# Folding key totals to 16 rows by a third accumulating transfer, stacking them half as wide, and giving the first value projection another bank

## The chip, the cores and the metric

The kernel runs on one core of one Trainium2 chip. The metric is the device time of one launch in microseconds (us), lower is better. Matmuls run on TensorE (PE in the profile), elementwise work on VectorE (DVE), exponentials and copies on ScalarE (ACT), masks on GpSimd (POOL), which also issues the accumulating transfers; SyncE (SP) issues the other transfers. Each engine works through a queue of its own in order, and the engines wait for each other through semaphores.

## The reference

`x` has the shape (32, 256, 32, 32) in float32. It is normalised per group, projected to queries, keys and values with 8 heads of 32 channels, and each of the 1024 positions attends to the positions strictly before it. The result is added to `x`.

```python
xf = _gn(x).reshape(B, C, S)                        # B=32, C=256, S=1024, 32 groups of 8 channels
q = einsum('oc,bcs->bos', q_w, xf) + q_b[None, :, None]
kv = einsum('oc,bcs->bos', kv_w, xf) + kv_b[None, :, None]
k, v = kv[:, :256], kv[:, 256:]                     # then split into 8 heads of 32
mask = tril(ones((S, S)), -1)
scores = einsum('bhqd,bhkd->bhqk', q, k) / sqrt(32)
attn = softmax(where(mask == 0, -10000.0, scores))
attn = where(mask == 0, 0.0, attn)
out = einsum('bhqk,bhkd->bhqd', attn, v)            # back to (B, 256, 32, 32)
return x + out
```

## The kernel before, in words

The kernel works through 32 batch elements, called batches here. A batch is ten *visits*: two groups of four heads, five visits for each group. A visit (`scores`) computes transposed score products for four heads into three PSUM tiles, two long ones `sT` and one short one `tri`, and ACT writes their exponentials to SBUF as `e` (two instructions on L443) and `eh` (L446). POOL then zeroes the forbidden parts (`mask`, L388). One visit later PE multiplies the exponentials by the values (`values`, tile `acc`, L472), and DVE adds the exponential tiles of several visits together (`add_keys`, L490), always into the `e` tile of the group's first or second visit. So each batch leaves four tiles of key totals, numbers n = 0 to 3: two groups by two halves of 512 queries. Each has 128 rows of partial totals and 4 x 512 columns (heads by queries).

The softmax denominator is the sum over those 128 rows. The kernel gets it like this:

- `fold(b, n, rows)` (L505): POOL issues an accumulating transfer that adds rows `rows` to `2 * rows` of the total onto rows 0 to `rows`. The first fold leaves 64 rows, the second leaves 32. A fold waits until the one before it on the same tile has landed.
- `stack(b, n)` (L511): SP copies the 32 remaining rows to partitions 32n to 32n + 31 of one tile `folded`.
- `sum_folded(b, heads)` (L518, L519): per head, DVE transposes the 128 x 512 slice in 32 x 32 blocks into `turned` and sums runs of 32 into `rows`. Four heads make four transposes and four sums a batch.
- `invert` (L547 to L559) takes reciprocals and writes them to DRAM, `spread_inverses` (L573) reads them back to the tile `rb`, spread over the partitions, and `finish` (L598 to L607) scales, adds bias and residual, and stores.

The `e` tiles of the first two visits of each group, where the totals stand, are taken from a ring of four buffers (tag `e0`). The buffer of a total is therefore written again by ACT exactly ten visits later, at the same visit of the next batch, and ACT must wait there until every fold and every stack of the old total has landed. The total n = 3 stands in the `e` tile of visit 6 of its batch, so ACT needs it back at visit 16, which is visit 6 of the next batch.

The order is written by hand. For each visit number i the main loop emits `scores(i)`, the first part of `values` of visit i - 1, the list `at[i]`, the second part of `values`, `add_keys`, and the list `after[i]`. Tables give the visits, counted from the batch's first: `SUMS` for the first fold of each n (the second fold comes one visit later), `STACK` for the stack, `PROJECT` and `PREPARE` for the next batch's projections and normalisation, `LOAD` for the input of the batch after that. A visit's tables can thus reach beyond 10, into the next batch.

Three pieces of machinery matter below. First, `with_scores(ahead)` makes SP wait for the semaphore `bank_free[0]`, which PE raises early in the score products of this visit, or of a visit ahead: the four input transfers `x` of visit 5 (L113) are tied in pairs, the first pair to visit 5's scores and the second to visit 6's. Second, POOL waits for the semaphore `begun` before the first fold of n = 1, and ACT raises it between its `e` and `eh` exponentials of visit 7. Third, ten-odd instructions of the next batch's normalisation share POOL's queue with folds and masks: the gather `eight` (L212), `rstd` (L250) and `shift` (L254); ACT's `xn` (L269) waits for `shift`.

A projection takes a PSUM bank either through `room`, half of an `sT` tile, or through `lone`, the bank of `acc`.

Of the kernel before, what the change touches and what calls it, by code (L numbers as in the profile page):

```python
# [17 lines left out]
P = 128  # L18
HD = 32
CPG = 8  # L20
HALF = 512
# [5 lines left out]
HALFBANK = HALF // 2  # L27
SHORT = 3 * P
ROW = 64
KEYS = 64  # L30


@with_exitstack
def tile_norm_attention_residual(
# [19 lines left out]
    nc = tc.nc  # L54
    B, C, H, W = x.shape
    S = H * W
    NG = C // P
    NB = S // P
    NH = S // HALF
# [22 lines left out]
        out=avg, in_=avg, pattern=[[-CPG, P // CPG], [0, CPG]],  # L82
# [3 lines left out]
        out=avg, in_=avg, pattern=[[CPG, P // CPG], [0, CPG]],  # L86
# [17 lines left out]
    def unshifted():  # L104
        live = {}
        bank_free = [tc.alloc_semaphore(f"bank_free_{k}") for k in range(2)]
        begun = tc.alloc_semaphore("begun")
        xpool = tc.alloc_tile_pool(name="xpool", bufs=4)
# [193 lines left out]
        def projections(b):  # L302

            def qk(n, g, hf, *bank):
                return lambda: project_qk(b, g, n, hf, *bank)

            def v(n, *bank):
                return lambda: project_v(b, n, *bank)

            early = [lone] if b == 0 else []  # L310
            return [
                qk(0, 0, 0, *early), qk(1, 0, 0), qk(0, 0, 1, *early), v(0), qk(1, 0, 1), qk(0, 1, 0, lone),
                qk(1, 1, 0), v(1), v(2), v(3), qk(0, 1, 1), qk(1, 1, 1, lone),
            ]

# [183 lines left out]
        def fold(b, n, rows):  # L499
            total = live["sum", b, *divmod(n, NH)]  # L500
            if (n, rows) == (1, HD):
                nc.gpsimd.drain()
            if (n, rows) == (1, 2 * HD):
                nc.gpsimd.wait_ge(begun, b + 1)
            nc.gpsimd.dma_start(out=total[:rows], in_=total[rows : 2 * rows], accum_op=ALU.add)  # L505

        def stack(b, n):
            if n == 0:
                live["folded", b] = work.tile([P, 4, HALF], F32, tag="folded", bufs=1, name=f"folded_{b}")
            total = live.pop(("sum", b, *divmod(n, NH)))  # L510
            nc.sync.dma_start(out=live["folded", b][n * HD : (n + 1) * HD], in_=total[:HD])  # L511

        def sum_folded(b, heads):
            if heads.start == 0:
                live["rows", b] = small.tile([P, ROW], F32, tag="rows", name=f"rows_{b}")
            for j in heads:
                turned = small.tile([P, HALF], F32, tag="turned", bufs=1, name=f"turned_{b}_{j}")
                nc.vector.transpose(turned, live["folded", b][:, j, :])  # L518
                nc.vector.tensor_reduce(  # L519
                    live["rows", b][:, j * HALF // HD : (j + 1) * HALF // HD],  # L520
                    turned.rearrange("p (k r) -> p k r", r=HD), AX.X, ALU.add,
                )

        def sum_keys(pd, e, of, start=True, stop=True):
            for j in range(4):
# [52 lines left out]
        def invert_here(b, n, within=slice(0, HALF)):  # L578


            if ("rb", b) not in live:
                live["rb", b] = work.tile([P, 4, HALF], F32, tag="folded", bufs=1, name="rb_last")
# [68 lines left out]
        N = NG * len(VISITS)  # L651
# [48 lines left out]
        at, after = {}, {}  # L700

        def when(i, f, where=at):
            where.setdefault(i, []).append(f)
# [16 lines left out]
        PROJECT = (-5, -4, -2, -3, 0, 1, 1, -1, 2, 4, 3, 6)  # L720
        PREPARE = (-12, -11, -10, -10, -9, -8, -7, -6, -4, -4, -3)
        SUMS = (4, 6, 8, 11)
        STACK = (6, 9, 11, 14)
        LOAD = 5
        SPREAD = (1, 1, 3, 4)
        FINISH = (N + 11, N + 11, N + 12, N + 13)
# [3 lines left out]
        with tc.manual_schedule(engines={ENG.PE, ENG.Activation, ENG.DVE, ENG.Pool, ENG.SP}):  # L730
# [11 lines left out]
                norm_channels(0, g)  # L742
            norm_mean(0)
            keep_busy(6, HD)
            odd = work.tile([P, 4, HALF], F32, tag="folded", bufs=1, name="less_mean")[:, 0, :]
# [32 lines left out]
            for b in range(B):  # L778
                first, last = b * N, b == B - 1
# [13 lines left out]
                if not last:  # L793
                    for n in every:
                        v = first + SUMS[n]
                        when(v, lambda b=b, n=n: fold(b, n, 2 * HD), at if n == 0 else after)
                        when(v + 1, lambda b=b, n=n: fold(b, n, HD), after)
                        when(first + STACK[n], lambda b=b, n=n: stack(b, n), at if n else after)
                    late = b == B - 2
                    v = first + N + (4 if late else 5)  # L800
                    when(v, lambda b=b: sum_folded(b, every[:2]), after)
                    when(v + 1, lambda b=b: sum_folded(b, every[2:]), after)
                    when(v + 2, lambda b=b: invert(b))
# [212 lines left out]
```

## Time and profile before

| what | value |
|---|---|
| median of 3 runs | 1808.08 us (1803.84 to 1809.35) |
| profiled execution, its own time | 1806.47 us |
| its span | 1803.3 us |
| granted TensorE clock | 0.999 |
| busy share PE / DVE / ACT / POOL | 99% / 93% / 82% / 46% |
| accumulating transfers from POOL | 124 of 512 KB and 124 of 256 KB |
| stack transfers from SP | 124 of 256 KB |

The profile is of one execution. A row of the timeline gives the start and the duration in us, the engine, the line, the operation, `out<-in` with buffer numbers left out, and in brackets how long the engine stood idle before it and which instruction ended that; SPq is SP's queue of transfers, whose duration is that of the issue. A row of the groups has the number of instructions, the busy time in us, and the mean of one in ns.

### The profile page before, as it was taken

The page shows a single profiled execution, that of the slowest core. Times are in us where ns is not written, and L with a number is a line of the kernel's source. Part 1 is how long each engine was busy: PE and PEld are TensorE (multiplying, and loading weights), DVE is VectorE, ACT ScalarE, POOL GpSimd, SP SyncE. Part 2 cuts the span into 40 slices and gives each one's busy share as a digit, 9 for nine tenths or more (in the row PEclk, how much of TensorE's full clock was granted, in tenths as well). Part 3 has the DMA queues.
Part 4 walks back from the last instruction along what each step waited for, and adds up shares of the span by engine and source line. Part 5 has one row for each costly group of instructions (what it writes and reads, how often), then busy time and mean ns, then how long its engine had stood idle before and what let it go on. Part 6 is the DMA issues. An engine that isn't in the chain of part 4 may idle for free.

```text
span 1803.3 us, 82014 instructions
## 1 busy us (share of the span) xinstructions
PE 1782.8 (99%) x37208; PEld 983.7 (55%) x37208; DVE 1682.6 (93%) x1852; ACT 1469.8 (82%) x1736; POOL 833.2 (46%) x935
## 2 busy tenths in 40 slices
PE   8999999999999999999999999999999999999998
PEld 5555555555555555555555555555555555555554
DVE  3789999999999999999999999999999999999996
ACT  5888888888888888888888888888888888888884
POOL 2445644444444444544544444545444444445541
PEclk9999999999999999999999999999999999999999
DMA  2566776666766767767667666676676676666662
GB/s 69 105 118 129 150 134 137 137 138 136 149 127 138 144 134 148 129 134 143 131 145 146 129 137 142 137 148 128 136 147 131 145 143 131 138 140 136 131 120 86
DMA packets 92771, 240.23 MB, mean 133 GB/s; under 512 B 26272, under 2 KB 27792, under 8 KB 76544
## 3 DMA queue, kind: packets, MB, share of 16 engines
q0 software_dynamic: 17360, 100.58, 39.0%
q1 hardware_dynamic: 74912, 134.28, 26.3%
q8 instruction: 292, 4.78, 1.1%
q14 instruction: 63, 0.52, 0.1%
q10 hardware_dynamic: 144, 0.07, 0.0%
HBM read 69.90 MB, written 34.95 MB: 58 GB/s over the span
## 4 chain that ended last, share of the span: by engine, by line
PE 57%; DVE 32%; issue 5%; DMA 3%; ACT 2%; DVEq 0%; SPq 0%; POOL 0%; ACTq 0%
DVE e L490 20%; PE acc L472 17%; PE pp L180 14%; PE tri L381 10%; PE sT L381 8%; PE ppv L180 7%; DVE turned L518 3%; DVE rows L519 3%; DVE rb L601 2%; DMA rb<-inverses 2%; DVE num L598 2%; ACT eh L446 2%; DVE st L196 1%; PE pd L526 1%; DVE mv L219 1%
## 5 line engine op out<-in xcount | busy, mean ns | idle before, releaser
L443 ACT ACTIVATE e<-sT 128x1024 f32<-128x1024 f32 x640 | 620.8, 1022 | 209.1 <-PE sT L381 204.3
L381 PE MATMUL tri<-q,k 32*64 32x128 f32 (+4 forms) x12416 | 550.4, 298 | 8.8 <-ACT eh L446 8.1
L381 PE MATMUL sT<-q,k 32*64 32x256 f32 (+1 forms) x7424 | 548.7, 462 | 1.2 <-issue 1.2
L381 PEld LDWEIGHTS tri<-q,k 32*64 32x64 f32 x12416 | 389.0, 131 | 185.9 <-issue 86.6
L388 POOL TENSOR_SCALAR_AFFINE_SELECT diagonal<-eh 128x512 f32<-128x512 f32 x384 | 363.2, 966 | 265.6 <-ACT eh L446 265.3
L180 PE MATMUL pp<-xn,wT 128*32 128x512 f32 (+1 forms) x4224 | 477.5, 582 | 0.0
L490 DVE TENSOR_TENSOR e<-e,eh 128x1536 f32<-128x1536 f32 x375 | 438.3, 1169 | 41.5 <-PE acc L472 28.2
L446 ACT ACTIVATE eh<-tri 128x1536 f32<-128x1536 f32 (+1 forms) x320 | 453.2, 1416 | 23.6 <-DVE e L490 23.6
L490 DVE TENSOR_TENSOR e<-e,e 128x2048 f32<-128x2048 f32 x187 | 447.4, 2393 | 6.4
L505 POOL DMA_DIRECT2D e<-e x248 | 206.5, 833 | 414.9 <-DMA e<-e 360.9
L472 PE MATMUL acc<-e,v 128*32 128x512 f32 x2560 | 338.5, 600 | 1.1 <-POOL diagonal L388 1.1
L381 PEld LDWEIGHTS sT<-q,k 32*64 32x64 f32 x7424 | 301.1, 131 | 15.2 <-issue 1.9
L180 PEld LDWEIGHTS pp<-xn,wT 128*32 128x32 f32 x4224 | 140.5, 109 | 270.6 <-issue 216.2
L490 DVE TENSOR_TENSOR e<-e,diagonal 128x1024 f32<-128x1024 f32 x187 | 245.0, 1310 | 19.4
L180 PE MATMUL ppv<-wT,xn 128*32 128x256 f32 x4032 | 240.6, 379 | 0.0
L472 PE MATMUL acc<-eh,v 128*32 128x384 f32 (+3 forms) x3072 | 198.7, 346 | 0.0
L472 PEld LDWEIGHTS acc<-eh,v 128*32 128x32 f32 x3072 | 97.0, 110 | 143.1 <-issue 120.6
L180 PEld LDWEIGHTS ppv<-wT,xn 128*32 128x32 f32 x4032 | 129.7, 110 | 69.0
L388 POOL TENSOR_SCALAR_AFFINE_SELECT e<-e 128x512 f32<-128x512 f32 x64 | 73.2, 1144 | 196.1 <-ACT e L443 196.1
L269 ACT ACTIVATE xn<-x,shift,rstd 128x256 f32<-128x256 f32 x248 | 135.4, 594 | 8.8 <-POOL shift L254 8.4
L601 DVE SCALAR_TENSOR_TENSOR rb<-num,v_bias_col,x 128x256 f32<-128x256 f32 x248 | 131.3, 569 | 4.4
L472 PEld LDWEIGHTS acc<-e,v 128*32 128x32 f32 x2560 | 62.8, 108 | 105.2 <-issue 94.6
(94 smaller groups left out, 1267.9 us busy)
## 6 DMA issues: line engine op xcount, KB each, us to landing
e<-e POOLq DMA_DIRECT2D x124, 512.0 KB, 6.2
x<-in_x_dram SPq DMA_DIRECT2D x124, 256.0 KB, 4.1
e<-e POOLq DMA_DIRECT2D x124, 256.0 KB, 4.7
folded<-e SPq DMA_DIRECT2D x124, 256.0 KB, 4.5
rb<-inverses SPq DMA_DIRECT2D x124, 256.0 KB, 5.0
out_dram<-rb SPq DMA_DIRECT2D x124, 256.0 KB, 3.8
x<-in_x_dram SPq DMA_DIRECT2D x2, 512.0 KB, 5.8
inverses<-inv_turned SPq DMA_DIRECT2D x31, 32.0 KB, 2.9
```

Source lines behind the costliest of these rows:

```text
L180: nc.tensor.matmul(out[part, cols], lhsT=lhsT[:, part], rhs=rhs[:, cols], start=start, stop=stop, skip_group_check=True)
L269: nc.scalar.activation(to, of, AF.Identity, bias=live["shift", b][:, g : g + 1], scale=rstd)
L381: return nc.tensor.matmul(to[c : c + KEYS, at : at + width], lhsT=live["k", b, g][rows, kb * P + c : kb * P + c + KEYS], rhs=live["q", b, ...
L388: nc.gpsimd.affine_select(out=to, in_=of, pattern=[[0, 4], [(1, -1)[odd], P]], compare_op=ALU.is_gt, fill=0.0, base=0, channel_multiplier= ...
L443: nc.scalar.activation(e[:, heads[a][0] : heads[a][1] + 1 : step, :], banks[a], AF.Exp)
L446: exp = nc.scalar.activation(eh[:, :, :wide], tri.rearrange("p (j q) -> p j q", q=SHORT)[:, :, :wide], AF.Exp)
L472: nc.tensor.matmul(acc[HD * j : HD * (j + 1), of], lhsT=live["v", b][:, kb, h * HD : (h + 1) * HD], rhs=e[:, j, :], start=first, stop=last ...
L490: nc.vector.tensor_add(to, to, tile_of(b, g, at))
L505: nc.gpsimd.dma_start(out=total[:rows], in_=total[rows : 2 * rows], accum_op=ALU.add)
L518: nc.vector.transpose(turned, live["folded", b][:, j, :])
L519: nc.vector.tensor_reduce(live["rows", b][:, j * HALF // HD : (j + 1) * HALF // HD], turned.rearrange("p (k r) -> p k r", r=HD), AX.X, ALU ...
L601: nc.vector.scalar_tensor_tensor(blocks(rb, s), blocks(num, s, (start + s) % 2 == 1), v_bias_col[:, g : g + 1], blocks(xt[:, g, cols], s), ...
```

## The change

- A third fold, `fold(b, n, TURN)` with `TURN = 16`, adds rows 16 to 31 onto rows 0 to 15. It is placed one visit after the second.
- `stack` copies the 16 rows in two transfers, one per 256 of the 512 queries, to partitions 32n + 16s. The tile (`stacked`) has 4 x 256 columns in place of 4 x 512.
- `sum_folded` handles two heads with one transpose and one sum of runs of 16: two transposes and two sums a batch in place of four and four.
- `STACK` goes from (6, 9, 11, 14) to (7, 10, 12, 15), and all four stacks stand in `after`; before, n = 1 to 3 stood in `at`.
- For the last batch but one, `sum_folded` and what follows come one visit later, as for the others.
- The first value projection of batch 0 takes its bank through `lone`. The scratch tiles of the last batch (`rb_last`) and of the beginning (`less_mean`) take other buffers, since the tile that they shared is smaller.

```diff
-                qk(0, 0, 0, *early), qk(1, 0, 0), qk(0, 0, 1, *early), v(0), qk(1, 0, 1), qk(0, 1, 0, lone),
+                qk(0, 0, 0, *early), qk(1, 0, 0), qk(0, 0, 1, *early), v(0, *early), qk(1, 0, 1), qk(0, 1, 0, lone),
...
-                live["folded", b] = work.tile([P, 4, HALF], F32, tag="folded", bufs=1, name=f"folded_{b}")
+                live["folded", b] = work.tile([P, 4, HALFBANK], F32, tag="stacked", bufs=1, name=f"folded_{b}")
             total = live.pop(("sum", b, *divmod(n, NH)))
-            nc.sync.dma_start(out=live["folded", b][n * HD : (n + 1) * HD], in_=total[:HD])
+            for s in range(2):
+                at = n * HD + s * TURN
+                nc.sync.dma_start(
+                    out=live["folded", b][at : at + TURN], in_=total[:TURN, :, s * HALFBANK : (s + 1) * HALFBANK]
+                )
...
-            for j in heads:
-                turned = small.tile([P, HALF], F32, tag="turned", bufs=1, name=f"turned_{b}_{j}")
-                nc.vector.transpose(turned, live["folded", b][:, j, :])
-                nc.vector.tensor_reduce(
-                    live["rows", b][:, j * HALF // HD : (j + 1) * HALF // HD],
-                    turned.rearrange("p (k r) -> p k r", r=HD), AX.X, ALU.add,
-                )
+            turned = small.tile([P, HALF], F32, tag="turned", bufs=1, name=f"turned_{b}_{heads.start}")
+            nc.vector.transpose(turned, live["folded", b][:, heads.start : heads.stop, :].rearrange("p j q -> p (j q)"))
+            nc.vector.tensor_reduce(
+                live["rows", b].rearrange("p (j s k) -> p j k s", s=2, k=HALFBANK // HD)[:, heads.start : heads.stop],
+                turned.rearrange("p (j k s r) -> p j k s r", j=len(heads), s=2, r=TURN), AX.X, ALU.add,
+            )
...
-        STACK = (6, 9, 11, 14)
+        STACK = (7, 10, 12, 15)
...
                         when(v + 1, lambda b=b, n=n: fold(b, n, HD), after)
-                        when(first + STACK[n], lambda b=b, n=n: stack(b, n), at if n else after)
+                        when(v + 2, lambda b=b, n=n: fold(b, n, TURN), after)
+                        when(first + STACK[n], lambda b=b, n=n: stack(b, n), after)
                     late = b == B - 2
-                    v = first + N + (4 if late else 5)
+                    v = first + N + 5
```

SP's queue around visit 15 of batch 3 (visit 5 of batch 4), before. In the names the first number is the batch; `e_3_1_1` holds the total n = 3 of batch 3, `folded_3` is the stacked tile, and a queue entry waits for the semaphores in brackets.

```order
L511 DMA folded_3_3482<-e_3_1_1_3408 32x2048 [waits DMASW4_49,DMAHW2_49,DMASW3_49,Activation_49]
L607 DMA out_0_dram<-rb_2_3659 128x512 [waits DVE_49]
L113 DMA x_6_4240<-in_x_dram 128x512 [waits bank_free_0,DMAHW4_49]
L113 DMA x_6_4240<-in_x_dram 128x512
L113 DMA x_6_4240<-in_x_dram 128x512 [waits bank_free_0,DMAHW6_49]
L113 DMA x_6_4240<-in_x_dram 128x512 [waits DMAHW7_49]
L511 DMA folded_4_4345<-e_4_0_0_3760 32x2048 [waits DMASW6_49,DMASW5_49,DMAHW0_49,DVE_49,DMAHW2_49,Activation_49,Pool_49]
```

The same place after the change.

```order
L611 DMA out_0_dram<-rb_2_3668 128x512 [waits DMAHW1_49,DVE_49]
L114 DMA x_6_4253<-in_x_dram 128x512 [waits bank_free_0,DMAHW2_49]
L114 DMA x_6_4253<-in_x_dram 128x512
L114 DMA x_6_4253<-in_x_dram 128x512 [waits bank_free_0,DMAHW4_49]
L114 DMA x_6_4253<-in_x_dram 128x512 [waits DMAHW5_49]
L514 DMA folded_3_3601<-e_3_1_1_3418 16x4x256 [waits DMASW4_49,DMASW3_49,DMAHW6_49,DMASW2_49,Activation_49]
L514 DMA folded_3_3601<-e_3_1_1_3418 16x4x256 [waits DMAHW7_49]
L563 DMA inverses_3_4432<-inv_turned_3_4430 128x2x32 [waits DMAHW0_49,DVE_49]
```

The stack of n = 3 has moved from ahead of the four input transfers to behind them, and is now two transfers; the second pair of inputs waits for `bank_free_0` of visit 16's scores.

ACT's queue at visit 16 (visit 6 of batch 4), where the buffer of that total is written again, after the change; the order of these instructions is that of before.

```order
L444 ACTIVATE e_4_1_1_4283<-sT_4_1_1_0_4285 128x1024 [waits DMASW4_49,DMAHW6_49,DMASW3_49,DMAHW7_49,DMASW2_49,PE_49]
L444 ACTIVATE e_4_1_1_4283<-sT_4_1_1_1_4286 128x1024 [waits PE_49]
L447 ACTIVATE eh_4_1_1_4284<-tri_4_1_1_4287 128x4x320 [waits DVE_49,PE_49,Pool_49]
L284 ACTIVATE k_4_1_3901<-pp_4_1_1_1_4325,qk_bias_83 128x512 [waits PE_49]
L284 ACTIVATE k_5_0_4335<-pp_5_0_1_0_4336,qk_bias_83 128x512 [waits PE_49]
```

DMASW2, 3 and 4 are raised by the three folds, and DMAHW6 and 7 by the two stack transfers of `e_3_1_1` shown above; before, the wait was for two folds and one stack transfer.

POOL's queue from visit 7 of batch 3 to visit 2 of batch 4, before.

```order
L505 DMA e_3_0_1_2971<-e_3_0_1_2971 32x2048
L388 AFFINE_SELECT diagonal_3_1_3_3651<-eh_3_1_3_3599 128x4x128 x2
L505 DMA e_3_1_0_3323<-e_3_1_0_3323 64x2048
L505 DMA e_3_1_0_3323<-e_3_1_0_3323 32x2048
L388 AFFINE_SELECT e_4_0_0_3760<-e_4_0_0_3760 128x4x128
L399 MEMSET e_4_0_0_3760 1x4
L388 AFFINE_SELECT eh_4_0_0_3761<-eh_4_0_0_3761 128x4x128
L212 DMA eight_5_3832<-each_5_3830,group_of_78 128x192
L388 AFFINE_SELECT diagonal_4_0_1_3873<-eh_4_0_1_3835 128x4x128 x2
L505 DMA e_3_1_1_3408<-e_3_1_1_3408 64x2048
L388 AFFINE_SELECT diagonal_4_0_2_3973<-eh_4_0_2_3921 128x4x128 x2
L505 DMA e_3_1_1_3408<-e_3_1_1_3408 32x2048
```

The same stretch after the change.

```order
L506 DMA e_3_0_1_2981<-e_3_0_1_2981 16x2048
L506 DMA e_3_1_0_3334<-e_3_1_0_3334 64x2048
L506 DMA e_3_1_0_3334<-e_3_1_0_3334 32x2048
L389 AFFINE_SELECT e_4_0_0_3769<-e_4_0_0_3769 128x4x128
L400 MEMSET e_4_0_0_3769 1x4
L389 AFFINE_SELECT eh_4_0_0_3770<-eh_4_0_0_3770 128x4x128
L506 DMA e_3_1_0_3334<-e_3_1_0_3334 16x2048
L213 DMA eight_5_3844<-each_5_3842,group_of_78 128x192
L389 AFFINE_SELECT diagonal_4_0_1_3885<-eh_4_0_1_3847 128x4x128 x2
L506 DMA e_3_1_1_3418<-e_3_1_1_3418 64x2048
L389 AFFINE_SELECT diagonal_4_0_2_3984<-eh_4_0_2_3932 128x4x128 x2
L506 DMA e_3_1_1_3418<-e_3_1_1_3418 32x2048
```

Two third folds have come in: one of n = 1 ahead of the first fold of n = 2, and one of n = 2 ahead of the gather `eight`.

More of the change, by code (lines that the diff above doesn't have):

```diff
@@ L29 @@
 ROW = 64
+TURN = 16
 KEYS = 64
@@ L581, in invert_here @@
             if ("rb", b) not in live:
-                live["rb", b] = work.tile([P, 4, HALF], F32, tag="folded", bufs=1, name="rb_last")
+                live["rb", b] = xpool.tile([P, NG, S], F32, tag="x", name="rb_last").rearrange("p g (hf q) -> p (g hf) q", hf=NH)
             k = (within.stop - within.start) // HD
@@ L744, in unshifted @@
             keep_busy(6, HD)
-            odd = work.tile([P, 4, HALF], F32, tag="folded", bufs=1, name="less_mean")[:, 0, :]
+            odd = work.tile([P, 4, HALFBANK], F32, tag="stacked", bufs=1, name="less_mean").rearrange("p j q -> p (j q)")[:, :HALF]
             live["less_mean"] = odd.rearrange("p (g n t) -> p g n t", g=NG, t=P)
```

## Prediction

> **What bounds the kernel now.** I read the page's busy shares first, then the table of waits, then the timeline of ACT, since its short exponential `eh` comes once a visit and marks the pace.
>
> ```profile
> PE 1782.8 (99%) x37208; PEld 983.7 (55%) x37208; DVE 1682.6 (93%) x1852; ACT 1469.8 (82%) x1736; POOL 833.2 (46%) x935
> POOL e L505 <- DMA e<-e: 360.9, 91, 8.4
> ACT eh L446 <- DVE e L490: 23.6, 28, 1.4
> ACT xn L269 <- POOL shift L254: 8.4, 18, 1.2
> ```
>
> PE is nearly never idle, so TensorE sets the pace, with DVE close behind. DVE makes ACT wait 28 times, once in nearly each batch, for 23.6 us in all. POOL stands 360.9 us in folds that wait for the fold before them to land.
>
> ```profile
> 135.17 1.46 ACT L446 ACTIVATE eh<-tri 128x1536 f32<-128x1536 f32 x1
> 173.92 1.46 ACT L446 ACTIVATE eh<-tri 128x1536 f32<-128x1536 f32 x1
> 178.84 1.46 ACT L446 ACTIVATE eh<-tri 128x1536 f32<-128x1536 f32 x1
> 189.66 1.45 ACT L446 ACTIVATE eh<-tri 128x1536 f32<-128x1536 f32 x1
> 853.21 1.46 ACT L446 ACTIVATE eh<-tri 128x1536 f32<-128x1536 f32 x1
> 892.15 1.46 ACT L446 ACTIVATE eh<-tri 128x1536 f32<-128x1536 f32 x1
> 898.02 1.45 ACT L446 ACTIVATE eh<-tri 128x1536 f32<-128x1536 f32 x1 [0.84 <-DVE e L490]
> 908.53 1.46 ACT L446 ACTIVATE eh<-tri 128x1536 f32<-128x1536 f32 x1
> ```
>
> The first four rows are batch 2 (visits 0, 7, 8 and the next batch's visit 0), the last four batch 15. Batch 2 takes 189.66 - 135.17 = 54.49 us, batch 15 takes 55.32 us: 0.8 us more, and the cause is visit 7, 4.92 us in the one and 5.87 us in the other, where ACT waits for DVE. DVE has just done `sum_folded` there. So DVE's share of the bound is worth about 0.8 us a batch; over the 28 waits, 28 x 0.8 = 22 us is the most that relief of DVE can bring.
>
> **The change, part by part.** First what it removes.
>
> ```profile
> L518 DVE STREAM_TRANSPOSE turned<-folded 128x512 f32<-128x512 f32 x124 | 87.9, 708 | 4.7 <-DMA folded<-e 1.4
> L519 DVE TENSOR_REDUCE rows<-turned 128x16 f32<-128x512 f32 x124 | 85.0, 686 | 4.3
> ```
>
> 62 transposes and 62 sums go, 62 x (0.708 + 0.686) = 86 us of DVE, 2.8 us a batch, just ahead of the visit-7 wait. That is more than the 0.8 us needed, so I take the wait as gone: -0.8 us a batch. (The sums that stay write 32 numbers where one wrote 16; if that doubled their 0.69 us, 1.4 us of the 2.8 would be left, still enough.)
>
> Next, the stack of n = 3, which the change moves behind the four input transfers of visit 15. These rows are batch 15's visit 6, that is visit 16 for the total of the batch before.
>
> ```profile
> 883.81 0.43 SPq L113 DMA_DIRECT2D x<-in_x_dram  x1
> 884.00 1.95 ACT L443 ACTIVATE e<-sT 128x1024 f32<-128x1024 f32 x2 [0.27 <-PE sT L381]
> 886.94 0.70 ACT L283 ACTIVATE k<-pp,qk_bias 128x512 f32<-128x512 f32 x1
> 884.54 3.64 PE L180 MATMUL pp<-xn,wT 128*32 128x512 f32 x32
> 888.00 1.04 PE L472 MATMUL acc<-e,v 128*32 128x512 f32 x8
> x<-in_x_dram SPq DMA_DIRECT2D x124, 256.0 KB, 4.1
> L511 SPq DMA_DIRECT2D folded<-e x124: 507/513/1567, 60.7 to 1757.5; - x124
> DMA to landing us min/median/max: 2.9/4.5/7.3
> 874.41 0.51 SPq L511 DMA_DIRECT2D folded<-e  x1
> ```
>
> The last row is the same stack before: SP sends it at 874.41, well ahead of ACT's exponentials at 884.00, which write the buffer that it reads. After the change SP can send it only when the last input transfer has been issued (883.81 + 0.43 = 884.24), since that one waits for this very visit's scores. Two issues of 0.51 us follow, the second beginning at 884.75. ACT's first exponential must wait until both have landed. The profile has 2.9 to 7.3 us from issue to landing for a stack of 256 KB, median 4.5. The two now hold 128 KB, but they stand right behind 512 KB of inputs on the same queue; I take the 4.1 us of an input transfer, the nearest neighbour. They land at 888.85, and ACT starts 888.85 - 884.00 = 4.85 us late. PE has little to do meanwhile: its `acc` at 888.00 waits for the copy `k` that ACT makes behind the exponentials, done at 886.94 + 0.70 = 887.64, so 0.36 us is slack. The second half of the 32 projections also needs the bank that the first exponential frees. PE loses 4.85 - 0.36 = 4.5 us a batch. The ends: 2.9 us to landing gives 3.3 us lost, 7.3 us gives 7.7.
>
> The Trainium skill ("DMA: Bandwidth & Descriptors", section "Anatomy of one DMA — SWDGE (gpsimd) path") puts a transfer at some 2.0 us fixed plus bytes over 436 GB/s, which gives an estimate of 2.15 us for 64 KB. By that the stack would land at 886.9 and PE lose 2.5 us; the earliest stack of this trace took 2.9 us.
>
> Then POOL's queue, where 124 third folds come in. Each is issued in about 0.84 us and waits for the second fold to land.
>
> ```profile
> e<-e POOLq DMA_DIRECT2D x124, 512.0 KB, 6.2
> e<-e POOLq DMA_DIRECT2D x124, 256.0 KB, 4.7
> 891.36 0.85 POOL L505 DMA_DIRECT2D e<-e  x1 [1.63 <-DVE turned L518]
> 898.37 0.80 POOL L505 DMA_DIRECT2D e<-e  x1 [3.46 <-DMA e<-e]
> 901.80 0.84 POOL L505 DMA_DIRECT2D e<-e  x1
> 909.83 0.79 POOL L505 DMA_DIRECT2D e<-e  x1 [7.18 <-DMA e<-e]
> 914.89 1.62 POOL L212 DMA_INDIRECT eight<-each,group_of  x1 [1.50 <-DMA each<-st]
> 918.34 0.91 POOL L505 DMA_DIRECT2D e<-e  x1
> 925.00 0.81 POOL L505 DMA_DIRECT2D e<-e  x1 [2.20 <-DMA e<-e]
> 927.21 0.20 POOL L254 TENSOR_TENSOR shift<-mean,rstd 128x2 f32<-128x2 f32 x1
> 927.44 1.09 ACT L269 ACTIVATE xn<-x,shift,rstd 128x256 f32<-128x256 f32 x2 [0.40 <-POOL shift L254]
> 928.64 1.94 ACT L443 ACTIVATE e<-sT 128x1024 f32<-128x1024 f32 x2
> ```
>
> The folds in these rows are first and second of n = 1, 2 and 3. The chain starts at `begun` (891.36, visit 7) and ends at `xn` in visit 13, for which ACT already waits 0.40 us. The second fold of n = 1 lands at 898.37 + 4.7 = 903.07; the third goes out then, and the first of n = 2 at 903.9 in place of 901.80: +2.1. If n = 2's first keeps its 909.83 - 901.80 = 8.03 us to the second, that one comes at 911.93, lands at 916.6, the third is issued by 917.5, and `eight` stands at 917.5 in place of 914.89: +2.6. From there all is handed on: masks, n = 3's folds, `shift`, `xn`, and the exponentials of visit 14 at 931.25 in place of 928.64. ACT has nothing else to do there, and PE needs the bank about 0.3 us after it is free, so PE loses 2.3 us against before, the 0.8 us of visit 7 swallowed. But the 8.03 us was measured beside the spread transfers `rb`; 2.1 us later the fold has less beside it. At the 6.2 us of the median the loss is 2.3 - 1.8 = 0.5. I take the middle, +1.4 us a batch, and as ends +2.3 and -0.8 (the chain catches up and only the gain of visit 7 shows).
>
> The other stacks come later too. That of n = 1 must land before visit 11's exponentials and is sent about 908, behind the third fold and a spread transfer; here a wait of 0 to 2 us is possible, but what PE loses there it does not lose again at visit 13, so no term of its own. Those of n = 0 and n = 2 have three visits or more. The removed 128 KB a stack and the added 128 KB a fold balance. The first value projection is 16 matmuls of 60 ns mean busy in all (below), once: 1 us either way. The tail's shift by a visit is bounded by the 5.2 us that DVE waits for `rb` in the whole run: I take +1 us, ends 0 and +5.
>
> ```profile
> L180 PE MATMUL ppv<-wT,xn 128*32 128x256 f32 x4032 | 240.6, 379 | 0.0
> DVE num L598 <- DMA rb<-inverses: 5.2, 4, 2.3
> ```
>
> **Sum.** The inputs of visit 5 exist for batches 2 to 31, so 29 stacks (batches 0 to 28) are caught behind them. 29 x (4.5 + 1.4) + 1 = 172 us. The profiled execution took 1806.47 us (span 1803.3 us), so 1978 us; on the median of 1808.08 us, which lies 1.6 us higher, 1980 us.
>
> **Rivals.** (a) The stack is late as said, but POOL's chain stays hidden, because transfers land sooner than in the rows above. Then 29 x (4.5 - 0.8) = 107 us, 1915 us. For it: POOL is busy only 46%. Against it: ACT waits for `shift` already. (b) Faster: the stack lands before ACT needs the buffer, and DVE's relief is all that shows. 1808 - 22 = 1786 us. It decides where PE loses less than the 0.8 us that DVE gives, so at a landing by 885.16 (884.00 + 0.36 + 0.8), 0.4 us after the second transfer is issued; for it there is only the chance that the queue or the ring of buffers is not as I read it, or that PE has more slack at visit 16 than 0.36 us. (c) The same, with POOL's chain giving the 0.8 us back: no change, 1808 us. (d) The stack lands as late as its slowest, 7.3 us: 29 x (7.7 + 1.4), 2072 us; its 7 us rows overlap other transfers, as this one would.
>
> **How the numbers follow.** Forecast 0.5 (1980 us), (a) 0.3, (b) 0.08, (c) 0.03, (d) 0.09. About 0.3% (5 us) is what a measurement here can tell from no change. Slower: 0.5 + 0.3 + 0.09 = 0.89; same 0.03; faster 0.08. Low end: 3.3 - 0.8 = 2.5 us a batch, 73 us, 1881, so 1880 us. High end: 5.6 us for the stack (5.2 us to landing, a quarter of the way from the median 4.5 to the slow end 7.3) plus 2.3, 7.9 x 29 = 229, 2037, so 2040 us.
>
> **What would show it.** Right: ACT's `e` at visit 6 of each batch stands idle some 5 us, ended by the stack's transfer; SP sends the stack right behind the fourth `x`; PE's idle time rises by 100 us and more; ACT's wait for `shift` grows from 8.4 us to 50 us or more; the wait of `eh` for DVE (23.6 us) is gone; transposes and sums fall to 62 each. Wrong: the exponentials of visit 6 start as before, or batches keep 55 us. A PE loss at visit 16 well under 3 us would say that small stacks land faster than any here; a loss at visit 13 of nothing would say that folds do.

## The result, and the profile after

| | before | after |
|---|---|---|
| median | 1805.78 us (1803.84 to 1809.35) | 2090.57 us (2084.66 to 2096.59) |
| ratio to before | | 1.157 (95% interval 1.155 to 1.160) |
| span of the profiled execution | 1803.3 us | 2087.9 us |
| granted TensorE clock | 0.999 | 0.953 |

The change makes the kernel 285 us slower. The direction and the place were as forecast; the size was not, and the time lies above the range (1880 to 2040 us).

The first lines of the page after, with the busy time, share and instructions of each engine, and the chain that ended last by engine:

```profile
span 2087.9 us, 82518 instructions
PE 1854.7 (89%) x37208; PEld 990.2 (47%) x37208; DVE 1551.4 (74%) x1728; ACT 1465.4 (70%) x1736; POOL 812.5 (39%) x1059
...
PE 65%; DMA 15%; ACT 7%; issue 6%; POOL 3%; SPq 2%; DVE 2%; POOLq 0%; ACTq 0%; DVEq 0%
```

No engine is busy throughout any more: PE has fallen from 99% to 89%, every other engine too, and 15% of the chain is now transfers, where it was 3%. The table of waits after (who waited, for what, us in total, times, longest) names them:

```profile
POOL e L506 <- DMA e<-e: 465.8, 146, 8.3
ACT e L444 <- DMA folded<-e: 287.3, 57, 8.7
PE pp L181 <- ACT e L444: 193.5, 55, 6.9
DVE turned L522 <- DMA folded<-e: 65.9, 30, 7.4
ACT xn L270 <- POOL shift L255: 18.5, 25, 3.2
```

ACT waits 57 times, nearly twice a batch, for a stack to land, 287.3 us in all, and PE waits behind it. ACT's wait of `eh` for DVE is gone. The wait for `shift` has grown only from 8.4 to 18.5 us.

Batch 15 shows where the two waits are. First ACT's `eh`, of visits 0, 1, 5, 6, 7 and the next batch's 0 (start and duration in us):

```profile
983.77 1.46 ACT L447 ACTIVATE eh<-tri 128x1536 f32<-128x1536 f32 x1
991.90 1.24 ACT L447 ACTIVATE eh<-tri 128x1280 f32<-128x1280 f32 x1
...
1013.75 1.46 ACT L447 ACTIVATE eh<-tri 128x1536 f32<-128x1536 f32 x1
1025.70 1.24 ACT L447 ACTIVATE eh<-tri 128x1280 f32<-128x1280 f32 x1
1033.34 1.46 ACT L447 ACTIVATE eh<-tri 128x1536 f32<-128x1536 f32 x1
...
1049.07 1.46 ACT L447 ACTIVATE eh<-tri 128x1536 f32<-128x1536 f32 x1
```

The batch takes 1049.07 - 983.77 = 65.30 us, where it took 55.32. I call the time from one `eh` to the next the interval of the earlier visit. Interval 5 is 1025.70 - 1013.75 = 11.95 us, interval 0 is 8.13 us, interval 6 is 7.64 us. The same differences, as medians over batches 2 to 29, in all the kernels of this study (the last column is the sum of the ten medians; 1 to 10 are the kernels of the experiments below):

| kernel | 0 | 1 | 2 | 3 | 4 | 5 | 6 | 7 | 8 | 9 | ten together |
|---|---|---|---|---|---|---|---|---|---|---|---|
| before | 5.37 | 6.14 | 4.92 | 5.51 | 5.29 | 5.40 | 6.14 | 5.93 | 4.89 | 5.61 | 55.2 |
| after | 7.42 | 6.14 | 4.92 | 5.51 | 5.29 | 12.11 | 7.24 | 4.92 | 5.53 | 5.29 | 64.3 |
| 1: before, last stack behind inputs | 5.37 | 6.14 | 4.92 | 5.50 | 5.29 | 12.18 | 6.84 | 4.91 | 5.53 | 5.29 | 62.0 |
| 2: after, last stack ahead | 8.15 | 6.87 | 5.06 | 5.50 | 5.29 | 5.86 | 6.14 | 4.92 | 5.53 | 5.29 | 58.6 |
| 3: as 2, stack n = 1 ahead too | 7.56 | 6.84 | 5.03 | 5.50 | 5.29 | 5.86 | 6.14 | 4.92 | 5.53 | 5.28 | 58.0 |
| 4: after, PE kept busy | 7.20 | 6.66 | 5.04 | 5.51 | 5.28 | 12.05 | 6.14 | 4.92 | 5.53 | 5.29 | 63.6 |
| 5: before, half the sums | 5.37 | 6.14 | 4.92 | 5.50 | 5.29 | 5.40 | 6.14 | 4.92 | 5.53 | 5.29 | 54.5 |
| 6: after, ring of five | 5.37 | 6.93 | 6.33 | 6.45 | 5.05 | 5.46 | 6.14 | 5.64 | 4.90 | 5.60 | 57.9 |
| 7: as 6, both stacks ahead | 5.37 | 6.98 | 6.75 | 6.44 | 5.05 | 5.45 | 6.14 | 4.92 | 5.53 | 5.29 | 57.9 |
| 8: as 7, later folds n = 2 | 5.37 | 6.14 | 7.83 | 4.90 | 5.61 | 5.40 | 6.14 | 4.92 | 5.53 | 5.29 | 57.1 |
| 9: as 8, later folds n = 3 | 5.37 | 6.14 | 4.92 | 5.51 | 5.61 | 5.39 | 6.14 | 5.36 | 6.54 | 5.29 | 56.3 |
| 10: as 9, later folds n = 1 | 5.37 | 6.14 | 7.29 | 4.89 | 5.61 | 5.40 | 6.14 | 4.92 | 6.17 | 5.29 | 57.2 |

After against before: +6.7 us in interval 5, +1.1 in interval 6, +2.05 in interval 0, and -0.7 in intervals 7 to 9 together. That is 9.15 us a batch by the medians. Over batches 2 to 29 the starts of `eh` have moved by 269 us (9.6 us a batch, the mean being above the medians), by 6.7 us before them and by 8.6 us in the last two batches and the tail. Kernel 9's profiled execution was a slow one, 1873.6 us against 1838.8 to 1861.8 us in the five others, so its row, and whatever is read from that trace below, may show more loss than the kernel usually has.

The stall in interval 5, in the timelines of SP, ACT and PE after:

```profile
1013.79 3.76 SPq L114 DMA_DIRECT2D x<-in_x_dram  x3
1017.73 2.12 SPq L514 DMA_DIRECT2D folded<-e  x2
1018.37 1.48 SPq L514 DMA_DIRECT2D folded<-e  x1
...
1023.87 1.94 ACT L444 ACTIVATE e<-sT 128x1024 f32<-128x1024 f32 x2 [7.08 <-DMA folded<-e]
...
1017.67 1.92 PE L181 MATMUL pp<-xn,wT 128*32 128x512 f32 x16
1024.95 3.64 PE L181 MATMUL pp<-xn,wT 128*32 128x512 f32 x16 [5.36 <-ACT e L444]
1028.37 1.86 PE L473 MATMUL acc<-e,v 128*32 128x512 f32 x8
```

SP sends the two halves of the stack right behind the last input transfer (1013.79 + 3.76 = 1017.55). The second begins to be issued at 1018.37, and ACT, which needs the buffer, starts 5.50 us later, after 7.08 us of idling; PE stands 5.36 us. Then the clock. These are stretches of 4 us with the busy time (and number of instructions) of PE, PEld, DVE, ACT and POOL, the granted clock, the DMA engines' share, and GB/s:

```profile
1018.00:1022.00 4.00, 1.59 (x16) 0.26 (x8) 3.86 (x3) 0.00 (x0) 0.04 (x1) 1.00 0.97 203
1022.00:1026.00 4.00, 1.05 (x8) 0.39 (x12) 2.62 (x4) 2.13 (x3) 0.00 (x0) 0.65 0.11 22
1026.00:1030.00 4.00, 4.00 (x24) 0.58 (x13) 2.33 (x6) 2.86 (x5) 1.96 (x3) 0.50 0.30 33
1030.00:1034.00 4.00, 4.00 (x130) 2.93 (x130) 3.43 (x3) 3.31 (x5) 0.81 (x1) 1.00 0.13 17
```

While the stack was on its way the DMA engines were 0.97 busy. And after 5.36 us without matmuls PE is granted half the clock for some 5 us: sixteen projections at 1024.95 take 3.64 us, while the sixteen at 1017.67, ahead of the stall, had taken 1.92. The stall of interval 0 in the same batch leaves PE without matmuls for 1.56 us, and there the granted clock stays at 1.00.

The durations of what the change touches, after (DMA issues with median us from issue to landing; groups with mean ns):

```profile
e<-e POOLq DMA_DIRECT2D x124, 128.0 KB, 4.2
folded<-e SPq DMA_DIRECT2D x248, 64.0 KB, 5.3
L522 DVE STREAM_TRANSPOSE turned<-folded 128x512 f32<-128x512 f32 x62 | 44.1, 712 | 66.9 <-DMA folded<-e 65.9
L523 DVE TENSOR_REDUCE rows<-turned 128x32 f32<-128x512 f32 x62 | 42.7, 688 | 2.2
```

In the median a 64 KB stack lands no sooner than the 256 KB one did (5.3 us against 4.5). The 62 transposes and 62 sums are gone, and those that stay cost what they cost before.

### The profile page after: what moved, and what is told of

Read it like the earlier page. It is cut to its first block, busy times and chain, and to the rows that moved or that the text cites. A ratio compares the mean times of both kernels' runs of the same rounds, so it can differ in the third digit from the quotient of the medians.

```text
span 2087.9 us, 82518 instructions
## 1 busy us (share of the span) xinstructions
PE 1854.7 (89%) x37208; PEld 990.2 (47%) x37208; DVE 1551.4 (74%) x1728; ACT 1465.4 (70%) x1736; POOL 812.5 (39%) x1059
## 4 chain that ended last, share of the span: by engine, by line
PE 65%; DMA 15%; ACT 7%; issue 6%; POOL 3%; SPq 2%; DVE 2%; POOLq 0%; ACTq 0%; DVEq 0%
PE acc L473 21%; PE pp L181 15%; DMA folded<-e 11%; PE tri L382 11%; PE ppv L181 9%; PE sT L382 9%; ACT e L444 4%; DMA e<-e 3%; DVE e L491 2%; ACT eh L447 2%; SPq L514 1%; POOL diagonal L389 1%; SPq L114 1%; POOL e L506 1%; ACT q L284 1%
## 5 line engine op out<-in xcount | busy, mean ns | idle before, releaser
L444 ACT ACTIVATE e<-sT 128x1024 f32<-128x1024 f32 x640 | 620.6, 1022 | 514.4 <-DMA folded<-e 287.3
L181 PE MATMUL pp<-xn,wT 128*32 128x512 f32 (+1 forms) x4224 | 539.3, 634 | 193.6 <-ACT e L444 193.5
L506 POOL DMA_DIRECT2D e<-e x372 | 309.1, 876 | 684.0 <-DMA e<-e 465.8
L491 DVE TENSOR_TENSOR e<-e,eh 128x1536 f32<-128x1536 f32 x375 | 417.0, 1112 | 188.1 <-PE acc L473 174.0
L382 PE MATMUL tri<-q,k 32*64 32x128 f32 (+4 forms) x12416 | 543.3, 298 | 2.9 <-issue 1.6
L389 POOL TENSOR_SCALAR_AFFINE_SELECT diagonal<-eh 128x512 f32<-128x512 f32 x384 | 289.7, 786 | 400.5 <-ACT eh L447 400.4
L491 DVE TENSOR_TENSOR e<-e,e 128x2048 f32<-128x2048 f32 x187 | 429.6, 2297 | 6.4
L473 PE MATMUL acc<-e,v 128*32 128x512 f32 x2560 | 351.7, 621 | 24.5 <-ACT q L284 22.6
L491 DVE TENSOR_TENSOR e<-e,diagonal 128x1024 f32<-128x1024 f32 x187 | 237.4, 1270 | 19.8 <-DVE e L491 0.5
L602 DVE TENSOR_TENSOR num<-num,rb 128x512 f32<-128x512 f32 x124 | 87.8, 708 | 82.6 <-DMA rb<-inverses 82.6
L270 ACT ACTIVATE xn<-x,shift,rstd 128x256 f32<-128x256 f32 x248 | 135.5, 596 | 18.7 <-POOL shift L255 18.5
L220 DVE BATCH_NORM_AGGREGATE mv<-eight 128x2 f32<-128x96 f32 x62 | 32.1, 560 | 144.1 <-DMA eight<-each,group_of 144.1
```

Source lines behind the costliest of these rows:

```text
L181: nc.tensor.matmul(out[part, cols], lhsT=lhsT[:, part], rhs=rhs[:, cols], start=start, stop=stop, skip_group_check=True)
L220: nc.vector.bn_aggr(live["mv", b][:, g, :], live["eight", b][:, :, g, :])
L270: nc.scalar.activation(to, of, AF.Identity, bias=live["shift", b][:, g : g + 1], scale=rstd)
L382: return nc.tensor.matmul(to[c : c + KEYS, at : at + width], lhsT=live["k", b, g][rows, kb * P + c : kb * P + c + KEYS], rhs=live["q", b, ...
L389: nc.gpsimd.affine_select(out=to, in_=of, pattern=[[0, 4], [(1, -1)[odd], P]], compare_op=ALU.is_gt, fill=0.0, base=0, channel_multiplier= ...
L444: nc.scalar.activation(e[:, heads[a][0] : heads[a][1] + 1 : step, :], banks[a], AF.Exp)
```

## The experiments

Each kernel is named by its number in the table above.

**1. The place in SP's queue, by itself.** This is the kernel before with one edit: the stack of n = 3 is issued behind the inputs of visit 15.

```diff
-                        when(first + STACK[n], lambda b=b, n=n: stack(b, n), at if n else after)
+                        behind = n == 3 and b < B - 2
+                        when(first + STACK[n] + behind, lambda b=b, n=n: stack(b, n), at if n and not behind else after)
```

> The kernel before with one edit: the stack of n = 3 (one transfer of 256 KB, no third fold, four transposes and four sums as before) stands behind the four input transfers of visit 15 for batches 0 to 29. Theory Q: the place in the queue alone makes most of the loss: ACT waits for the stack at visit 6 of 29 batches, visits 5 and 6 take 18 to 20 us together, 29 x 6.5 to 8.5 = 190 to 245 us, so 1995 to 2050 us. Rival P (it is the third fold and the small pieces): under 1 us a batch, below 1835 us.

Measured: 2009.79 us, ratio 1.110 (1.106 to 1.113). Its waits, and the same place in its batch 15:

```profile
ACT e L443 <- DMA folded<-e: 209.1, 29, 7.7
PE pp L180 <- ACT e L443: 159.0, 29, 6.0
...
986.86 1.80 SPq L511 DMA_DIRECT2D folded<-e  x1
993.60 1.94 ACT L443 ACTIVATE e<-sT 128x1024 f32<-128x1024 f32 x2 [7.61 <-DMA folded<-e]
```

That is inside the 1995 to 2050 us expected. So this one transfer's place costs 203 us, with two folds, one 256 KB stack and all the old transposes. It takes 29 waits of 7.2 us, one for each batch that has inputs behind it, as counted in the prediction. Interval 5 is as long as after the change (12.18 us against 12.11), so neither the halving of the stack nor the third fold makes that stall, and the halving did not shorten it.

**2 and 3. The changed kernel with stacks ahead.** In 2 the stack of n = 3 goes back to where visit 15's inputs stand behind it; in 3 the stack of n = 1 also goes a visit earlier.

```diff
-                        when(first + STACK[n], lambda b=b, n=n: stack(b, n), after)
+                        when(first + STACK[n], lambda b=b, n=n: stack(b, n), at if n == 3 else after)
```
```diff
-        STACK = (7, 10, 12, 15)
+        STACK = (7, 9, 12, 15)
```

> The changed kernel with the stack of n = 3 put back ahead of the four input transfers of visit 15 (into the list `at`; one visit later than in the kernel before). Theory Q (the queue: the stack waits behind inputs that are tied to the very visit whose exponentials need its buffer): visits 5 and 6 go back from 19.4 us together to 11.5 us, 29 x 7.8 = 226 us come back, 2090 -> about 1865 us; what is left over the kernel before is the 2 us of visit 0, where the stack of n = 1 is late. Rival P (64 KB transfers in pieces of 1 KB are slow wherever they stand, or the third fold lands too late): the wait of ACT for the stack stays or moves by a visit, and less than 100 us come back, over 1990 us.

> As the run before, and the stack of n = 1 too moved one visit sooner, to visit 9, ahead of the spread transfer that is tied to visit 10's scores. Theory Q: visit 0 goes back from 7.4 to 5.4 us as well, the wait for DVE at visit 7 stays gone, and the kernel is 28 x 0.8 = 22 us faster than the one before: about 1784 us. Rival C (POOL's chain of folds, each waiting for the landing of the last, then shows at visits 12 to 14, as my prediction had it): 1.4 to 2.3 us a batch, 1805 + 40 to 70 = 1845 to 1875 us, with ACT waiting for `shift` some 60 us or more.

Measured: 1910.29 us, ratio 1.056 (1.052 to 1.059), and 1891.52 us, ratio 1.047 (1.045 to 1.049). The first gives 180 of the 285 us back, less than the 226 expected: intervals 5 and 6 are nearly as before, but interval 0 has grown from 7.42 to 8.15 us and interval 1 from 6.14 to 6.87 (why interval 1 grew stays open). The second misses both theories, 1784 us and 1845 to 1875 us; ACT's wait for `shift` is 8.7 us, not the 60 of the rival. It gains little over the first: interval 0 stays at 7.56 us, though the stack of n = 1 stood two visits from the exponentials that wait for it. In kernel 3's trace, POOL, SP and ACT around that place in one batch:

```profile
1392.59 0.82 POOL L506 DMA_DIRECT2D e<-e  x1 [0.16 <-DVE turned L522]
1400.78 0.81 POOL L506 DMA_DIRECT2D e<-e  x1 [3.06 <-issue]
1406.42 1.66 POOL L506 DMA_DIRECT2D e<-e  x2 [3.35 <-DMA e<-e]
...
1410.71 1.35 SPq L514 DMA_DIRECT2D folded<-e  x2
...
1415.91 1.94 ACT L444 ACTIVATE e<-sT 128x1024 f32<-128x1024 f32 x2 [3.78 <-DMA folded<-e]
```

The first three rows are the first, second and third fold of n = 1 (the last row of them holds the first of n = 2 too). They go out at 1392.59, 1400.78 and 1406.42, each behind the landing of the one before (7.0, 5.4 and 4.2 us after their issue), then the stack at 1410.71, whose second half lands at 1415.73, and ACT gets its buffer at 1415.91. From `begun` (visit 7) to visit 11 there are four landings in a row, and they do not fit. The place in SP's queue is not what binds here; the third fold is, which the stack follows by 0.1 us. In kernel 1, with the old place of this stack and no third fold, interval 0 is 5.37 us, as before; no run leaves out the third fold alone.

**4. The clock.** In the changed kernel the projection that stands ahead of the stall is computed four times over into the same place, so that PE has work in it: 1392 matmuls more.

```diff
-            for cc in range(NG):
+            again = 4 if (n, g, hf) == (1, 1, 1) and 0 < b < B - 2 else 1
+            for cc in list(range(NG)) * again:
```

> The changed kernel, where the projection that PE makes at visit 6 just ahead of the wait is computed four times over (the last pass counts, each pass 16 matmuls, 1.8 us at the full clock), in batches 1 to 29. PE does 5.4 us more work a batch, inside its 5.4 us of idle time. Theory K (the granted clock falls to half after PE has stood idle, 0.50 in the window 1026 to 1030 us of the changed kernel, and the matmuls behind the wait take twice as long): with PE busy through the wait the clock stays near 1, the 16 matmuls behind it take 1.9 us in place of 3.6, and the run is 29 x 1.5 to 2.5 = 45 to 70 us faster than the changed kernel, 2020 to 2045 us. Rival W (the clock doesn't matter, the wait for the transfer alone sets the time): the same time as the changed kernel, 2090 us, or more if the added passes run over.

Measured: 2066.43 us, ratio 1.144 (1.141 to 1.146): with more work it is 24 us faster than the changed kernel, about half of the 45 to 70 us expected. The 4 us behind the stall of batch 15 (columns as above) are at full clock:

```profile
1010.00:1014.00 4.00, 3.28 (x67) 1.21 (x65) 3.49 (x7) 4.00 (x7) 1.96 (x3) 1.00 0.02 4
```

Interval 6 is back at 6.14 us, the stall itself is as long as before (12.05). So the half clock after an idle PE is a cost of its own, 1.1 us a batch in interval 6; intervals 0 and 1 together became 0.3 us longer, for a reason that stays open, and the 24 us are what is left.

**5. What relief of DVE is worth.** The kernel before, with two of its four transposes and sums left out. The denominators of two heads in four are set to 1 instead, so that part of the computation is missing.

```diff
-            for j in heads:
+            if heads.start == 0:
+                nc.vector.memset(live["rows", b], 1.0)
+            for j in heads[:1]:
```

> The kernel before with two of its four transposes and two of its four sums a batch left out (the totals of two heads in four are set to 1, so the output lacks their denominators); one fill of 128 x 64 numbers is added. Nothing else moves. This is the DVE relief of the change alone, 2.7 us a batch. Theory R (DVE sets only the wait of visit 7): visit 7 falls to 4.92 us and batches to 54.5 us, 28 x 0.8 = 22 us faster, about 1784 us, and no more. Rival (DVE holds PE elsewhere too): 1765 us or less. Rival (the wait of visit 7 is not DVE's backlog): 1800 us or more.

Measured: 1787.88 us, ratio 0.989 (0.988 to 0.991). Interval 7 falls from 5.93 to 4.92 us and the batch to 54.5. That is 19 us, close to the 22 expected, and it is all that this relief of DVE brings by itself.

**6 and 7. Another buffer.** The ring of `e0` gets five buffers instead of four, so a total's buffer is next written some visits later. (The last batch's sums move to a tile of another pool to make room.) In 7 the stacks of n = 1 and n = 3 stand as in kernel 3 besides.

```diff
-            e = epool.tile([P, 4, HALF], F32, tag="e0" if i < 2 else "e", bufs=4 if i < 2 else 3, name=f"e_{name}")
+            e = epool.tile([P, 4, HALF], F32, tag="e0" if i < 2 else "e", bufs=5 if i < 2 else 3, name=f"e_{name}")
```

> The changed kernel with a ring of five `e0` buffers in place of four (8 KB a partition; to make room, the small `den` tiles of the last batch lie in a free input buffer). SP's and POOL's queues are as in the changed kernel; ACT now gets a buffer whose total was stacked one number earlier, so that at visit 16 it waits for the stack of n = 2 (sent at visit 12) and at visit 11 for that of n = 0. Theory Q (the stacks are late for the buffer, and for nothing else): the waits of ACT for `folded` (287 us) and of visits 0, 5 and 6 go, DVE's relief shows, 1806 - 22 = about 1785 us. Rival C (the longer chain of folds in POOL's queue, with its masks and `shift`, or DVE's wait for the late stack, then sets the pace): 0.5 to 2 us a batch stay, 1800 to 1850 us. Rival P (transfers disturb each other, the ring is not the cause): over 1950 us.

> The run before with the stacks of n = 1 and n = 3 also put ahead in SP's queue (visit 9, and visit 15 ahead of the inputs). Theory Q: the buffers no longer depend on the stacks, so the place in the queue matters only for DVE, which no longer waits for the stack of n = 3 before it sums: 1785 us, within 5 us of the run before. Rival C: the same loss as there, or more, since SP now stands in front of the third folds.

Measured: 1913.22 us, ratio 1.059 (1.056 to 1.062), and 1905.25 us, ratio 1.055 (1.050 to 1.059). Both lie above the 1785 us of the theory, and kernel 6 above the 1800 to 1850 of its rival too. No ACT wait for a stack is left in either, and intervals 0, 5 and 6 are as before, as the theory had it. But intervals 1 to 3 have become slow, by 3.1 us together in kernel 6 and by 3.6 in kernel 7. Kernel 7's waits, and its POOL queue at visits 9 to 11 of a batch:

```profile
POOL e L506 <- DMA e<-e: 594.0, 174, 7.5
ACT xn L270 <- POOL shift L255: 51.1, 30, 2.5
PE acc L473 <- POOL e L400: 27.6, 20, 3.4
...
1017.06 1.66 POOL L506 DMA_DIRECT2D e<-e  x2 [3.25 <-DMA e<-e]
1025.41 0.76 POOL L506 DMA_DIRECT2D e<-e  x1 [6.69 <-DMA e<-e]
1025.92 0.90 POOL L389 TENSOR_SCALAR_AFFINE_SELECT e<-e 128x512 f32<-128x512 f32 x1
...
1030.36 0.81 POOL L506 DMA_DIRECT2D e<-e  x1 [2.80 <-DMA e<-e]
1031.47 1.09 POOL L213 DMA_INDIRECT eight<-each,group_of  x1 [0.31 <-issue]
```

POOL stands 6.69 us in the second fold of n = 2, which waits for the first to land, and the mask of visit 10 (`e`, 1025.92) and the gather `eight` (1031.47) stand behind it. PE then waits for the fill (L400) that POOL makes right behind that mask, and ACT waits for `shift`. This is the chain on POOL that the prediction had put at 1.4 us a batch; with the stalls for the stacks out of the way intervals 1 to 3 lose more than twice that.

**8, 9 and 10. The order on POOL.** All three keep five buffers. In 8 the second and third fold of n = 2 come one visit later, so that POOL makes visit 10's mask first, and `shift` goes ahead of n = 3's second fold. In 9 n = 3's folds are later too, in 10 n = 1's as well.

```diff
+                        v += n in (2,)
                         when(v + 1, lambda b=b, n=n: fold(b, n, HD), after)
                         when(v + 2, lambda b=b, n=n: fold(b, n, TURN), after)
...
-                        (first + n, after) if k == 1 else first + n for k, n in enumerate(PREPARE)
+                        (first + n, after) if k in (1, 2, 5) else first + n for k, n in enumerate(PREPARE)
...
-        STACK = (7, 9, 12, 15)
+        STACK = (7, 9, 13, 15)
```

Kernel 9 has `n in (2, 3)` in that first line, kernel 10 `n > 0` and `STACK = (7, 10, 13, 15)`.

> Ring of five and stack n=3 ahead of the inputs, as in the run that took 1905 us, and of the folds n=2 the second and third each one visit later, so that POOL makes visit 10's masks ahead of the wait for the first; shift goes ahead of the second fold n=3. Theory (what is left over before is POOL: its in-order queue stands at a fold that waits for the fold ahead of it, and masks, eight and shift stand behind): visits 11 to 13 fall from 6.98, 6.75 and 6.44 us to near 6.1, 4.9 and 5.5, so 3 us a batch come back and the time is 1785 to 1820 us. Rival (visits 11 to 13 are slow because of what DVE does there, or because the transfers take longer beside each other): 1890 to 1910 us, whatever the order on POOL.

> As the run beside it, and the second and third folds of n=3 one visit later too. Theory (POOL's queue): shift is free of the folds n=3, and visit 13 is as in the kernel before; 1780 to 1815 us, not slower than the run beside it, unless the last stack is late for the transposes at visit 15, which costs DVE alone. Rival (not POOL): 1890 to 1910 us.

> As the run that took 1847 us, with the second and third folds of n=1 one visit later too, behind visit 8's masks, and stack n=1 at visit 10. Theory (POOL's queue): visit 8, the slowest against before there (6.54 us against 4.89), falls to near 5 us, about 1.2 us a batch, and the time is 1795 to 1825 us, near the kernel before. Rival (visit 8's loss is the longer way of the data, not the masks behind a waiting fold): 1840 to 1875 us.

Measured: 1872.69 us, ratio 1.038 (1.036 to 1.040); 1847.10 us (1842.71 without the profiled execution), ratio 1.023 (1.019 to 1.026); 1880.11 us, ratio 1.042 (1.038 to 1.046). Against the 1905 us of kernel 7, later folds (with the stack of n = 2 behind them) and an earlier `shift` bring 33 us in kernel 8 and 58 in kernel 9 (63 by its second figure), with the same transfers and the same work on DVE: the order of POOL's queue is a cause. None came as low as expected. Kernel 9's waits, then kernel 10's:

```profile
POOL e L506 <- DMA e<-e: 243.8, 111, 4.6
DVE num L604 <- DMA rb<-inverses: 75.2, 29, 6.5
```
```profile
POOL e L506 <- DMA e<-e: 248.5, 83, 4.6
DVE num L604 <- DMA rb<-inverses: 165.9, 31, 8.5
```

In kernel 9 POOL's waits in folds are less than half of kernel 7's, intervals 1 to 3 are as in the kernel before, and the loss has moved to interval 8 (6.54 us against 4.89). Kernel 10 was to cure it. It took only 0.4 us off it (6.54 to 6.17), and interval 2 became slow. In its trace DVE waits 165.9 us for `rb`, the last step of the same denominators. Both theories' times were missed there, if the second by little (1795 to 1825, and 1840 to 1875 us).

Kernel 8 has the same slow interval 2, 7.83 us against 4.92, and its trace shows what it waits for. Two lines of its waits, then DVE and ACT in visits 2 and 3 of its batch 15:

```profile
ACT eh L447 <- DVE e L491: 69.8, 35, 3.4
PE tri L382 <- ACT eh L447: 51.1, 29, 2.8
...
891.19 1.39 DVE L604 TENSOR_TENSOR num<-num,rb 128x512 f32<-128x512 f32 x1 [3.43 <-DMA rb<-inverses]
897.13 2.56 DVE L491 TENSOR_TENSOR e<-e,eh 128x1536 f32<-128x1536 f32 x2
898.99 1.45 ACT L447 ACTIVATE eh<-tri 128x1536 f32<-128x1536 f32 x1 [2.20 <-DVE e L491]
```

DVE stands 3.43 us for `rb`, comes to its additions of `eh` only at 897.13, and ACT's next `eh` waits 2.20 us for DVE, with PE behind it. Kernel 10's batch 15 has the same chain, with 4.34 and 1.85 us. So the denominators now come too late for DVE: in the whole run it waits 102.4 us for `rb` in kernel 8, where it was 5.2 us before. No run gave DVE its `rb` earlier, so the share of this in the time is not shown, and what holds kernel 9 above the kernel before stays open. No version of the change beat the kernel before.

## Why the prediction was right and wrong

- **Relief of DVE: right.** At most 22 us were put down for it; experiment 5 gives 19. The wait at visit 7 is gone, and the sums that write 32 numbers did not become longer (688 ns against 686).
- **The stack of n = 3: right in mechanism, place and count, wrong in size. This is the term that failed.** It stood at 4.5 us a batch and measured 6.7 in interval 5. "I take the 4.1 us of an input transfer, the nearest neighbour" was the wrong choice: from the issue of the second half to ACT's start it took 5.50 us. The two issues were slower too: the second began 0.64 us behind the first where 0.51 was priced, and 0.82 us behind the end of the last input's issue. The 4.1 us is a median over 124 inputs in all sorts of company, while in batch 15 this stack was on its way together with the last two inputs of 256 KB and a fold, with the DMA engines 0.97 busy. In kernel 2, where it stands ahead of the inputs, its second half lands 3.7 us after its issue in the median, here 5.5; that speaks for the company as the cause, though no run changed it alone. Better rows were to hand before the change. The trace gives the landing of 63 of the 124 old stacks, and their medians differ by number: 3.7 us for n = 0, 7.0 for n = 1, 2.9 for n = 2, and 5.7 for n = 3 itself. One of these, issued at 984.58:

```profile
folded<-e SPq DMA_DIRECT2D x1, 256.0 KB, 5.8
```

With 5.7 in place of 4.1 the term would have been 6.1 us. Rival (d), at 0.09, had 7.7 us for the stack and 2072 us in all. That this comes near the measured time is luck: its stack was slower than the 6.7 us measured, it held POOL's 1.4 us, which did not show, and it lacked the stack of n = 1 and the clock.

- **The Trainium skill's estimate** ("DMA: Bandwidth & Descriptors", section "Anatomy of one DMA — SWDGE (gpsimd) path") gave 2.15 us for 64 KB. Its fit is for transfers that GpSimd issues, while SP issues the stacks. Here the median of 248 such stacks was 5.3 us. The measurement decides; a fixed price and a size did not tell when these transfers landed among others.
- **The clock: not priced.** PE's 5.36 us of idling bring a granted clock of 0.50 behind it. Experiment 4 puts that at 1.1 us a batch in interval 6, and gains 24 us in all. The Trainium skill ("TensorE: Matmul & The Clock Gate", Part 1: The HAM clock gate) states that the clock is halved after at least one idle window of about 3.4 us, until PE has been busy for at least one such window. The rows of batch 15 agree: 5.36 us idle, then some 5 us of matmuls at 0.50.
- **The stack of n = 1: wrong.** "A wait of 0 to 2 us is possible" was right in size (2.05 in interval 0), but it was given no term, on the ground that PE would not lose the same again at visit 13. It was a loss of its own, 28 x 2.05 = 57 us over batches 2 to 29. Its four landings in a row could have been added up from rows that the prediction showed.
- **POOL's chain: real, but not where it was put.** After the change intervals 3 and 4 are unchanged, and the wait for `shift` is 18.5 us, not the 50 and more that were to show it: as I read it, the stalls for the stacks give POOL the time to catch up. The +1.4 a batch was thus no part of this result. Experiments 6 and 7, without these stalls, uncover it, at 3.1 to 3.6 us a batch. Reordering POOL takes it out of intervals 1 and 3 in kernel 8 and out of 1 to 3 in kernel 9, but part of the loss comes back elsewhere.
- **The first value projection and the tail.** They stood at +1 us together; the last two batches and the tail lost 8.6. Of these 3.6 are the wait for the stack of n = 1, which batches 30 and 31 have as well (intervals 0 of 6.64 and 7.70 us against 5.37); the cause of the rest stays open.
- **The sum.** Forecast 4.5 + 1.4 = 5.9 us a batch; measured, by the medians, 6.7 + 1.1 + 2.05 - 0.7 = 9.15. The largest part of the difference is the stack of n = 3 (+2.2), then that of n = 1 (+2.05, in place of the 1.4 of POOL's chain), then the clock (+1.1). The DVE gain, -0.7, was netted in the +1.4, so it comes off here: 2.2 + 0.65 + 1.1 - 0.7 = 3.25 us.

## What to carry to other kernels

When a transfer that reads a ring's buffer is moved, note what its queue waits for just ahead of it and when the buffer is written next: here one place in SP's queue cost 203 us with nothing else changed. Price its landing by the rows of that very transfer, or of one in the same company, not by the median of a neighbour, and add up every landing in a chain to the visit that needs it. Relief of an engine is worth only the wait that others have for it (19 us here, of 86 us saved on DVE), and 5 us of an idle PE cost again in the clock behind them.

## What the runs showed of the hardware that was not expected

A stack of 64 KB took 5.3 us to land in the median, one of 256 KB had taken 4.5, and the medians of the latter ran from 2.9 us (n = 2) to 7.0 (n = 1): the size alone did not set it. The granted clock stood at 0.50 after 5.36 us without matmuls and came back after some 5 us of matmuls, so that a kernel with 1392 more matmuls ran 24 us faster.
